# Reordering the last 512 tokens of a Mamba input stage: all convolutions first, two a slot, then the gates

## The chip, the cores and the metric

The kernel runs on one core of a Trainium2 chip. A core has TensorE (PE in the profile; its weight loads are PEld), VectorE (DVE), ScalarE (ACT), GpSimd (POOL), and SyncE (SP), whose queue here issues most of the DMAs. Each engine works through its own instructions in order and waits on semaphores for the others. The metric is the device time of one execution in microseconds; before the change the median of three runs is 3320.36 us (3317.36 to 3326.46).

## The reference, cut to what matters

The whole is one decoder layer over 4 x 1024 tokens of width 512: a Mamba block with an MLP, then a cross attention, then a dense layer with routed low-rank experts. The change lies in the first part of the Mamba block:

```
xz = rmsnorm(x) @ in_proj_w.T
u, z = split(xz, 2)                       # 1024 channels each
u_act = silu(conv4(u) + conv_b)           # causal, 4 taps, per channel
proj = u_act @ x_proj_w.T                 # 32 for dt, 16 for B, 16 for C
dt = softplus(dt_r @ dt_proj_w.T + dt_proj_b)
dA = exp(dt * A);  dBu = dt * B * u_act   # 16 states per channel
h_t = dA_t * h_{t-1} + dBu_t;  y = sum_n h * C + u_act * D
y = y * silu(z);  out = y @ out_proj_w.T
```

softplus(v) is computed as relu(v) + ln(1 + exp(-|v|)), with the rounding error of the sum 1 + e taken back out.

## The kernel before, in words

The 4096 tokens are cut into eight chunks of 512 (`c` = 0 to 7, `NC` = 8), and the 1024 inner channels into eight blocks of 128 (`j` = 0 to 7, `KI` = 8). There are two stages that matter here.

**The input stage** (`mamba_in`, line 357) makes u, z, dt and dt*u for every chunk and puts them into DRAM as `pk`. It is a software pipeline written out by hand in *slots*, one for each (c, j), numbered 8c + j in what follows. A slot has four phases. `slot(c, j)` (line 630) runs what is due in phase 0, issues the 12 matmuls of `conv(j)`, runs phase 1, issues the 12 matmuls of `gate(j)`, and runs phases 2 and 3. `at(d, phase, f)` puts a step d slots later. The distances stand in the table `AP` at the top of the file.

- `conv(j)` (479): matmuls into PSUM `ps_in`; one slot later ScalarE makes the first tap (`conv_start`, `cv`) and VectorE the other three (`conv_taps`, plus three narrow ones from the `halo` in odd chunks); two slots later ScalarE makes tanh (`conv_tanh`, which takes a new tile `u`, eight buffers, each for two blocks) and VectorE `conv_end`; three slots later comes `x_proj`.
- `gate(j)` (534): matmuls, then tanh on ScalarE and a multiply on VectorE one slot later, and a DMA of z.
- After `x_proj` of the eighth block, `project` (549) copies the projection to `pr` and `bc`, and eight `dt(b)` (574) follow at the distances `AP["b"]`: (2,2), (2,2), (3,2), (3,2), (6,2), (6,3), (7,2), (7,3). Each `dt` is one matmul into one of two PSUM buffers `ps_dt`; one slot later ScalarE makes four passes (`dt_exp`, 598: `e` = |v|, `r` = relu, exp into `ps_dt`, and `q` = 1 + exp), then VectorE makes `dt_round` (607), GpSimd `dt_add` (595). After each four of them ScalarE makes the logarithm (`dt_log`, 610), VectorE `dt_sum`, GpSimd `dt_u` (622), which is the last reader of the tile `u`. `q` and `r` have two buffers, each for four blocks.

So the softplus of chunk 6 falls into slots 60 to 69 and that of chunk 7 into slots 68 to 77. After slot 63 no matmul of `conv` or `gate` is left; the slots 64 to 72 are run alone (`while n < 9`), and the remaining five are handed over as a generator, `rest()` (685).

**The scan** (`scan_mlp`, line 695) then goes through 256 steps (chunk, half of the channels, state), four quarters each. GpSimd makes dt*u*B (`times_b`, tile `hs`), ScalarE exp(dt*A) (`exp`, tile `da`), VectorE the scan itself, TensorE the transposes (`ps_h`), and ScalarE, VectorE or GpSimd the sums over states (`acc`, `hc`, `hz`). The first four steps are interleaved with what is left of the input stage: every other quarter draws one slot of `rest()`. From step 40 on, the output projection and the MLP run beside the scan.

**What sets the order.** All instructions of an engine that come from `mamba_in` keep their program order (`InOrder`, line 291), and so do all of `scan_mlp`; the scheduler may interleave these two sequences by its own estimate of times. DMAs of the SP queue are not held in that order. The scan's tiles `pk` and `b` lie in the memory of the weights `wu`, and the three buffers of `hs` in the memory of `wz`, so that GpSimd's first `hs` must wait for the last `gate` matmul. Every instruction goes through the helper at line 311, so the profile names tiles and not lines.

Of the kernel before, what the change touches and what calls it, by code (L numbers as in the profile page):

```python
# [10 lines left out]
F32 = mybir.dt.float32  # L11
F32R = mybir.dt.float32r
I32 = mybir.dt.int32
AF = mybir.ActivationFunctionType
ALU = mybir.AluOpType
# [4 lines left out]
P = 128  # L20
# [3 lines left out]
DI, KI = 1024, 8  # L24
NS = 16
DTR = 32
T = 512
NT = T // P
NC = N // T
# [3 lines left out]
AP = {  # L33
    "cv": (1, 1),
    "cw": (1, 3),
    "ut": (2, 1),
    "uu": (2, 2),
    "up": (3, 0),
    "zt": (1, 1),
    "zz": (1, 3),  # L40
    "th": (1, 0),
# [99 lines left out]
for g, first in enumerate((4, 6)):  # L141
    for n in range(1, 16):
        for t in range(4):
            i = 4 * (n - 1) + t
# [182 lines left out]
class Slots:  # L327
# [5 lines left out]
    def at(self, d, phase, f, *args):  # L333
        self.due.setdefault((self.now + d, phase), []).append(lambda: f(*args))

    def run(self, phase):
        for f in self.due.pop((self.now, phase), ()):
            f()
# [18 lines left out]
def mamba_in(tc, cn, a, dr, sx):  # L357
# [5 lines left out]
    nc = pin  # L363
    ident, pvec = cn["ident"], cn["pvec"]
    slots = Slots()
    at, run = slots.at, slots.run
    with ExitStack() as ctx:
# [4 lines left out]
        tp = ctx.enter_context(open_pool(tc, "a_t", bufs=2))  # L372
# [66 lines left out]
        class Step:  # L439
# [39 lines left out]
            def conv(self, j):  # L479
# [5 lines left out]
                at(*AP["uu"], self.conv_end, j, cv)  # L485
                at(*AP["up"], self.x_proj, j)

            def conv_start(self, j, ps, cv):
                cv.append(tp.tile([P, T], F32, tag="cv", name="cv", bufs=2))
                nc.scalar.activation(  # L490
                    cv[0], ps, AF.Identity, bias=vec(V_CB + j), scale=vec(V_CW + 4 * j + 3)
                )
# [29 lines left out]
            def x_proj(self, j):  # L522
                if j == 0:
                    self.xp = qp.tile([P, T], F32, tag="xp", name="ps_xp")
                nc.tensor.matmul(
                    self.xp, wxp[:, j], self.u[j // 2][:, j % 2], start=j == 0, stop=j == KI - 1
                )
                if j == KI - 1:
                    at(1, 0, self.project)
                    at(1, 0, self.project_rest)  # L530
                    for b in range(KI):
                        at(*AP["b"][b], self.dt, b)

            def gate(self, j):

# [3 lines left out]
                at(*AP["zz"], self.gate_end, j, z, ps)  # L539

            def gate_tanh(self, j, z, ps):
                z.append(tp.tile([P, T], F32, tag="z", name="z", bufs=2))
                nc.scalar.activation(z[0], ps, AF.Tanh, scale=0.5)

            def gate_end(self, j, z, ps):
# [28 lines left out]
            def dt(self, j):  # L574


                g, i = divmod(j, 2 * 2)
                if i == 0:
                    self.qr[g] = [
                        sp.tile([P, 2 * 2, T], F32, tag=t, name=t, bufs=4 // 2) for t in "qr"  # L580
                    ]
                q, r = (t[:, i] for t in self.qr[g])
                ps = pd.tile([P, T], F32, tag="dt", name="ps_dt")
                nc.tensor.matmul(ps, wdt[:, j * P : (j + 1) * P], self.pr, start=True, stop=True)
                e = []
                at(*AP["d1"], self.dt_exp, j, ps, e, q, r)
                at(*AP["d2"], self.dt_round, ps, e, q)
                at(*AP["d3"], self.dt_add, e, r)
                if i == 2 * 2 - 1:
                    at(*AP["d4"], self.dt_log, g)  # L590
                    for jp in range(2):
                        at(*AP["d5"][jp], self.dt_sum, 2 * g + jp)
                        at(*AP["d6"][jp], self.dt_u, 2 * g + jp)
# [4 lines left out]
            def dt_exp(self, j, ps, e, q, r):  # L598

                e.append(sp.tile([P, T], F32, tag="e", name="e", bufs=3))  # L600
                (e,) = e
                nc.scalar.activation(e, ps, AF.Abs, bias=vec(V_DTB + j))
                nc.scalar.activation(r, ps, AF.Relu, bias=vec(V_DTB + j))
                nc.scalar.activation(ps, e, AF.Exp, scale=-1.0)
                nc.scalar.activation(q, ps, AF.Identity, bias=1.0)

            def dt_round(self, ps, e, q):
                nc.vector.scalar_tensor_tensor(e[0], q, -1.0, ps, ALU.add, ALU.subtract)
# [19 lines left out]
                put(nc, dr, self.c, jp, 1, q)  # L628

        def slot(c, j):  # L630
            run(0)
            if c < NC:
                now[0].conv(j)
            run(1)
            if c < NC:
                now[0].gate(j)
            run(2)
            if c < NC:
                if j == 0 and c + 1 < NC:
                    n = now[1] = Step(c + 1)  # L640
                    for t in range(NT):
                        at(*AP["nm"][t], n.moments, t)
                        at(*AP["nx"][t], n.normed, t)
                    for k in range(KD):
                        at(*AP["t"][k], n.turn, k)
                    at(*AP["nr"], n.scale)
                if later and (c, j) >= WS:
                    Weight(*later.pop(0))
                if j == KI - 1:
                    now.pop(0)  # L650
                    now.append(None)
            run(3)
            slots.now += 1
# [23 lines left out]
                    load_in(wz, DI, j // 3, [nc.gpsimd, nc.vector])  # L677
                slot(c, j)
        assert not later
        n = 0  # L680
        while n < 9:
            slot(NC, n)
            n += 1

    def rest():
        n = 9
        while slots.due:
            slot(NC, n)
            n += 1
            yield  # L690
# [1383 lines left out]
```

## Time and profile before

| | |
|---|---|
| median of three runs | 3320.36 us |
| the profiled execution | 3321.16 us, span 3319.4 us, mean granted TensorE clock 0.955 |
| busy over the span | PE 90%, DVE 86%, POOL 74%, ACT 62% |
| last `conv` matmuls / last `gate` matmuls start | 499.81 us / 503.01 us |
| `project` of chunk 7 on ScalarE | 521.88 us |
| GpSimd's first `hs` / VectorE's first scan | 534.33 us / 536.70 us |
| GpSimd's last `q<-r,u` (the last work of the input stage on it) | 593.46 us |

The shares over the span are averages over stages with different limits: the input stage until about 506 us, a handover between the stages until about 597 us, the scan alone until about 760 us, then the scan with the MLP, and last the attention. The change touches only slots 56 to 77, which is 451.7 us to about 596 us, so that stretch has to be read by itself.

### The profile page before, as it was taken

How to read it: one execution, taken by the hardware profiler on the slowest of the kernel's cores; microseconds unless marked ns; L12 is line 12 of the kernel's file. 1: busy time of each engine (PE TensorE's matmuls, PEld its weight loads, DVE VectorE, ACT ScalarE, POOL GpSimd, SP SyncE). 2: the span in 40 equal slices, each digit the busy share in tenths (PEclk: the TensorE clock that was granted, in tenths of full speed). 3: DMA queues.
4: the chain of work that ended last, by engine and by line, in shares of the span. 5: the costliest groups of instructions: out<-in, count | busy, mean ns of one | idle time of the engine just before them, and what ended most of it. 6: DMA issues, size and time to landing. Idle time of an engine off the chain costs nothing.

```text
span 3319.4 us, 47302 instructions
## 1 busy us (share of the span) xinstructions
PE 2993.0 (90%) x15768; PEld 2366.4 (71%) x15768; DVE 2867.0 (86%) x4063; ACT 2043.6 (62%) x4000; POOL 2454.5 (74%) x2153
## 2 busy tenths in 40 slices
PE   7999894677899999999999998999999998999986
PEld 5767672565686786786786786786786887998875
DVE  6888887998999999999999999999983346889887
ACT  3778788775665566665566665566652336666642
POOL 1456547898999999999999999999972215667643
PEclk9999995678999999999999999999999999999998
DMA  4677745334666666666766765765757532112010
GB/s 161 221 260 241 256 175 173 99 111 166 210 207 193 216 203 191 222 203 188 230 196 184 238 190 183 241 191 179 234 171 231 161 108 93 52 39 65 30 39 32
DMA packets 478474, 562.79 MB, mean 170 GB/s; under 512 B 46006, under 2 KB 309814, under 8 KB 477974
## 3 DMA queue, kind: packets, MB, share of 16 engines
q1 hardware_dynamic: 464406, 526.21, 49.6%
q10 hardware_dynamic: 13824, 33.56, 2.9%
q8 instruction: 125, 2.05, 0.2%
q14 instruction: 119, 0.97, 0.1%
HBM read 430.18 MB, written 129.50 MB: 169 GB/s over the span
## 4 chain that ended last, share of the span: by engine, by line
PE 38%; DVE 26%; POOL 10%; issue 6%; ACT 5%; DMA 3%; SPq 0%; ACTq 0%; POOLq 0%; DVEq 0%
DVE hs L311 11%; PE ps_ab L311 10%; PE ps_h L311 5%; PE ps_o L311 5%; POOL hs L311 5%; PE ps_m L311 5%; DVE acc L311 5%; PE ps_s L311 3%; PE ps_b L311 2%; POOL acc L311 2%; DVE g L311 1%; ACT da L311 1%; PE ps_in L311 1%; PE ps_y L311 1%; PE ps_num L311 1%
## 5 line engine op out<-in xcount | busy, mean ns | idle before, releaser
L311 DVE TENSOR_TENSOR_SCAN hs<-da,hs 128x512 f32<-128x512 f32 x1024 | 1225.3, 1217 | 19.8 <-ACT da L311 19.4
L311 POOL TENSOR_TENSOR hs<-pk,b 128x1024 f32<-128x1024 f32 x512 | 1214.1, 2387 | 23.3 <-PE ps_h L311 14.9
L311 ACT ACTIVATE da<-pk,aneg 128x512 f32<-128x512 f32 x1024 | 706.2, 690 | 632.1 <-DVE hs L311 622.0
L311 PE MATMUL ps_ab<-xn,w 128*128 128x512 f32 x3072 | 832.6, 407 | 3.4 <-DVE xs L311 3.4
L311 PE MATMUL ps_h<-ident,hs 128*128 128x128 f32 x4096 | 693.0, 291 | 129.1 <-DVE hs L311 66.1
L311 PEld LDWEIGHTS ps_h<-ident,hs 128*128 128x128 f32 x4096 | 533.4, 148 | 371.0 <-DVE hs L311 112.2
L311 PEld LDWEIGHTS ps_ab<-xn,w 128*128 128x128 f32 x3072 | 547.8, 191 | 98.9 <-DVE xs L311 4.1
L311 DVE SCALAR_TENSOR_TENSOR acc<-ps_h,c,acc 128x512 f32<-128x512 f32 x598 | 439.8, 735 | 26.1 <-PE ps_h L311 20.7
L311 PE MATMUL ps_m<-w,gs 128*128 128x512 f32 x1536 | 418.4, 409 | 6.0 <-POOL gs L311 3.5
L311 POOL TENSOR_TENSOR acc<-acc,hc 128x512 f32<-128x512 f32 x232 | 298.9, 1288 | 68.3 <-ACT hc L311 67.1
L311 PEld LDWEIGHTS ps_m<-w,gs 128*128 128x128 f32 x1536 | 275.6, 192 | 55.4 <-POOL gs L311 5.5
L311 PE MATMUL ps_o<-wo,wy 128*128 128x512 f32 x512 | 247.1, 601 | 10.0 <-DMA wy<-y 8.8
L311 POOL TENSOR_TENSOR gs<-g,gs 128x512 fp32r<-128x512 f32 x128 | 164.9, 1288 | 79.8 <-ACT gs L311 79.5
L311 PE MATMUL ps_in<-xn,wu 128*128 128x512 f32 x768 | 217.5, 433 | 0.3 <-DVE xn L475 0.2
L311 PE MATMUL ps_in<-xn,wz 128*128 128x512 f32 x768 | 193.2, 400 | 8.2 <-DVE cv L311 4.1
L311 ACT ACTIVATE hc<-ps_h,c 128x512 f32<-128x512 f32 x288 | 193.1, 671 | 3.8 <-PE ps_h L311 3.8
L311 PEld LDWEIGHTS ps_in<-xn,wu 128*128 128x128 f32 x768 | 147.4, 193 | 58.8 <-issue 23.8
L311 POOL TENSOR_TENSOR pt<-pw,pt 128x512 fp32r<-128x512 f32 x48 | 67.3, 1402 | 161.8 <-ACT pt L311 133.8
L311 PEld LDWEIGHTS ps_in<-xn,wz 128*128 128x128 f32 x768 | 143.2, 189 | 43.4 <-ACT q L311 4.6
L311 DVE SCALAR_TENSOR_TENSOR g<-g,ps_ab 128x512 f32<-128x512 f32 x128 | 87.4, 683 | 85.3 <-ACT g L311 84.7
L311 DVE SCALAR_TENSOR_TENSOR cv<-ps_in,pvec,cv 128x509 f32<-128x509 f32 (+2 forms) x192 | 143.3, 746 | 4.8
L311 POOL TENSOR_TENSOR q<-qf,q 128x256 fp32r<-128x256 f32 x64 | 47.6, 744 | 127.4 <-ACT q L311 127.3
(251 smaller groups left out, 4982.6 us busy)
## 6 DMA issues: line engine op xcount, KB each, us to landing
w<-w SPq DMA_DIRECT2D x384, 512.0 KB, 5.3
b<-b SPq DMA_DIRECT2D x256, 256.0 KB, 4.3
pk<-pk SPq DMA_DIRECT2D x64, 512.0 KB, 5.8
w<-pt SPq DMA_DIRECT2D x48, 512.0 KB, 3.1
pk<-z SPq DMA_DIRECT2D x64, 256.0 KB, 2.3
pk<-u SPq DMA_DIRECT2D x32, 512.0 KB, 3.7
pk<-r SPq DMA_DIRECT2D x32, 512.0 KB, 4.6
pk<-q SPq DMA_DIRECT2D x32, 512.0 KB, 5.3
```

Source lines behind the costliest of these rows:

```text
L311: ins = f(*args, **kw)
```

## The change

In the last chunk (slots 56 on) the order of `conv` and `gate` changes. Slots 56 to 59 issue two `conv` each, slots 60 to 67 one `gate` each, in the place of one `conv` and one `gate` in each of the slots 56 to 63. Since two convolutions are under way at once, those with odd j take their `cv` tile from the two buffers of `z`, and the odd gates their `z` from those of `cv` (`tile`). The eight `dt` of chunk 6 come two a slot in slots 60 to 63 (they were in 60, 60, 61, 61, 64, 64, 65, 65). `project` of chunk 7 comes in slot 64, two slots after its last `x_proj`, and its `dt` come two a slot in slots 65 to 68 (they were in 68, 68, 69, 69, 72, 72, 73, 73). In chunks 6 and 7, `q` = 1 + e moves from ScalarE (`dt_exp`) to VectorE (`dt_one`). The slots run alone after slot 63 are five (64 to 68) in the place of nine, and the rest is four slots (69 to 72) in the place of five (73 to 77).

```diff
+            def tile(self, tag, other, j):
+                if self.c == NC - 1 and j % 2:
+                    tag = other
+                return tp.tile([P, T], F32, tag=tag, name=tag, bufs=2)
...
-                cv.append(tp.tile([P, T], F32, tag="cv", name="cv", bufs=2))
+                cv.append(self.tile("cv", "z", j))
...
-                    at(1, 0, self.project)
-                    at(1, 0, self.project_rest)
+                    last = self.c - (NC - 2)
+                    at(2 if last == 1 else 1, 0, self.project)
+                    at(2 if last == 1 else 1, 0, self.project_rest)
                     for b in range(KI):
-                        at(*AP["b"][b], self.dt, b)
+                        at(*(AP["b"][b] if last < 0 else (2 + last + b // 2, 2 + b % 2)), self.dt, b)
...
-                z.append(tp.tile([P, T], F32, tag="z", name="z", bufs=2))
+                z.append(self.tile("z", "cv", j))
...
                 at(*AP["d1"], self.dt_exp, j, ps, e, q, r)
+                if self.c >= NC - 2:
+                    at(*AP["d2"], self.dt_one, ps, q)
                 at(*AP["d2"], self.dt_round, ps, e, q)
...
-                nc.scalar.activation(q, ps, AF.Identity, bias=1.0)
+                if self.c < NC - 2:
+                    nc.scalar.activation(q, ps, AF.Identity, bias=1.0)
+            def dt_one(self, ps, q):
+                nc.vector.tensor_scalar(q, ps, 1.0, None, ALU.add)
...
         def slot(c, j):
+            i = KI * (c - (NC - 1)) + j
             run(0)
-            if c < NC:
+            if i < 0:
                 now[0].conv(j)
+            elif i < KI // 2:
+                now[0].conv(2 * i)
             run(1)
-            if c < NC:
+            if i < 0:
                 now[0].gate(j)
+            elif i < KI // 2:
+                now[0].conv(2 * i + 1)
+            elif i < KI // 2 + KI:
+                now[0].gate(i - KI // 2)
...
-                if j == KI - 1:
+                if j == KI - 1 and c + 1 < NC:
                     now.pop(0)
...
-        n = 0
-        while n < 9:
+        for n in range(5):
             slot(NC, n)
-            n += 1
...
-        n = 9
+        n = 5
```

## The prediction

> **What bounds the kernel now.** I read the page's 40 slices first, to find the stage; then the busy time by stage; then the timeline around the end of the slots; last GpSimd's groups in the handover. The slices show the dip that the change is aimed at (the seventh slice, 498 to 581 us):
>
> ```profile
> PE   7999894677899999999999998999999998999986
> DVE  6888887998999999999999999999983346889887
> ACT  3778788775665566665566665566652336666642
> POOL 1456547898999999999999999999972215667643
> PEclk9999995678999999999999999999999999999998
> ```
>
> The stretches 451.7 to 506 (slots 56 to 63), 506 to 534.3 (until GpSimd's first hs), 534.3 to 597 (the first scan steps, mixed with the rest of the input stage), and 597 to 760 (scan alone); columns are busy us per engine, granted clock, DMA share:
>
> ```profile
> 451.70:506.00 54.30, 53.98 (x221) 40.89 (x220) 47.24 (x77) 46.00 (x70) 22.28 (x16) 1.00 0.40 148
> 506.00:534.30 28.30, 9.38 (x18) 3.77 (x17) 13.88 (x18) 22.81 (x36) 16.61 (x9) 0.58 1.01 335
> 534.30:597.00 62.70, 27.28 (x94) 17.98 (x95) 54.12 (x45) 44.77 (x71) 57.71 (x35) 0.50 0.26 89
> 597.00:760.00 163.00, 128.65 (x728) 99.64 (x727) 159.76 (x160) 131.68 (x251) 153.49 (x74) 0.72 0.33 105
> ```
>
> TensorE is the limit to 506 (54.0 of 54.3), ScalarE with its chain of softplus in the second row (22.8 of 28.3), GpSimd in the third (57.7 of 62.7), VectorE in the fourth (159.8 of 163). GpSimd's timeline shows where the scan is held:
>
> ```profile
> 527.55 5.57 POOL L311 TENSOR_TENSOR q<-r,u 128x1024 f32<-128x1024 f32 x2 [3.44 <-DVE r L311]
> 533.09 1.27 POOL L311 TENSOR_TENSOR r<-r,e 128x512 f32<-128x512 f32 x1
> 534.33 13.88 POOL L311 TENSOR_TENSOR hs<-pk,b 128x1024 f32<-128x1024 f32 x6
> 548.17 3.72 POOL L311 TENSOR_TENSOR r<-r,e 128x512 f32<-128x512 f32 x3
> ```
>
> The groups of 534 to 598 (busy us and mean ns, then idle before and its releaser) show what the handover costs GpSimd, and VectorE's sums beside it:
>
> ```profile
> L311 POOL TENSOR_TENSOR hs<-pk,b 128x1024 f32<-128x1024 f32 x15 | 34.8, 2339 | 0.0
> L311 POOL TENSOR_TENSOR q<-r,u 128x1024 f32<-128x1024 f32 x4 | 10.3, 2583 | 5.0 <-DVE r L311 5.0
> L311 POOL TENSOR_TENSOR r<-r,e 128x512 f32<-128x512 f32 x8 | 10.0, 1262 | 0.0
> L311 DVE TENSOR_TENSOR r<-r,q 128x1024 f32<-128x1024 f32 x4 | 15.6, 3926 | 3.0 <-issue 3.0
> ```
>
> The first hs has no wait before it: it stands in GpSimd's queue behind chunk 6's last dt_u and a dt_add, not behind memory (the last gate matmuls were over at 505.97). From there GpSimd hardly rests until 595.89, where its steady row of hs begins. So the change is worth what it does to two things: when the first hs can start, and how much dt_add and dt_u is left for GpSimd after that.
>
> **The conv slots, 56 to 59.** The matmuls are the same 24 a slot, 5.6 us by the chain (two pieces of 2.8), so TensorE gains nothing here. VectorE pays: one conv is 2.31 (three taps) + 0.73 (halo) + 0.69 (conv_end) = 3.7 us, two are 7.5, against 4.4 for a conv and a gate (0.68). Its chain, from the conv_end at 457.82, where slot 57 begins: slot 57, 0.7 + 6.1 (taps and halo of two) + 1.4 (two dt_round of chunk 5) = 8.2; slot 58, 1.4 + 6.1 + 1.4 = 8.9; slot 59, 0.7 (project_rest) + 1.4 + 6.1 = 8.2, to 483. ScalarE has 7.9 in slot 58 and 8.5 in slot 59 beside it, of which 4.5 is the logarithm of chunk 5 with two table loads (500.17 to 504.69 shows one).
>
> **A new wait in slot 60.** `u` has eight buffers. The third tile of chunk 7 is now taken in slot 60, phase 1, by conv_tanh(4), and it needs the buffer whose last reader is chunk 5's dt_u(2), in slot 60, phase 2. Before, it was taken two slots later. dt_u(2) needs dt_sum(2) on VectorE (483 to 484.2), then 2.4 to 3.3 on GpSimd: about 487. Behind the waiting tanh on ScalarE stand the first taps of conv 6 and 7, for which VectorE waits. Then two conv_end, one stretched by GpSimd (2.85 in the timeline at 505.75, against 0.69), 3.5 us, and 6.1 of taps: 497. Without the wait it would be 494.
>
> **The gate slots, 60 to 67, and both softplus.** ScalarE sets the pace. One dt costs it 0.57 + 0.71 + 0.63 = 1.9 from start to start (before: 2.42 with q), one z 0.5, project 1.1, a logarithm 4.5. From 497: slot 61 tanh 0.6, z, two dt, 0.1: 5.0; slot 62, 4.3; slot 63 with a logarithm, 8.8; slot 64 with project, 5.4; slot 65, z and logarithm, 5.0; slot 66, 4.3. Sum 32.8, so the second dt of chunk 7 leaves ScalarE at 529.8. Then 1 + e and dt_round on VectorE (1.35), the dt matmul that waits for this PSUM buffer in TensorE's queue (0.3), and behind it the last gate, 2.8: over at 534.3 at full clock. That releases `wz`, so hs can start. GpSimd has by then chunk 6's dt_u (logarithm over at 524, sums, then 3.3 + 2.4 with one dt_add between) and dt_add of the first two dt.
>
> **The clock.** After the TensorE gap from 509.8 the granted clock was 0.55, and the dt matmul there took 0.80 in the place of 0.40. In slot 63 TensorE has about 3.3 of work in 8.8 us, so one or two gates run at half clock: 5.1 in the place of 2.8 (12 x 0.43). I count 1.7 us for that: first hs at 536. The Trainium skill, "TensorE: Matmul & The Clock Gate", section "What's actually happening", has the clock halved after an idle window of about 3.4 us and given back after as long a busy one; by that rule most gate slots, whose gaps are shorter, stay fast, and the sum would be 534 to 537. It speaks against thinning out the matmuls, as this change does, but not by much.
>
> **1 + e on VectorE.** No row shows this form (PSUM in, SBUF out). TENSOR_SCALAR on 128x512 from SBUF took 0.59 (x<-x,rms_r), a pass with a PSUM input 0.68 (z<-z,ps_in): 16 x 0.59 to 0.68 = 9.4 to 10.9 us onto VectorE, I take 0.6, since there is one input. ScalarE loses 16 x 0.598 = 9.6. Eight of these are in the gate slots, where VectorE has at most 6.4 a slot; of the others four come after 536, 2.4 us, in a stretch where VectorE was busy 54.1 of 62.7 and 11 of its 15.6 us of r<-r,q were stretching (1.2 alone, up to 7.45 beside GpSimd). If GpSimd stopped being the limit there, 2.4 us would be the price. The skill's "SBUF — State Buffer", "Who interferes with whom", says that only a VectorE instruction with two SBUF inputs, or in a two-port mode, is locked out by GpSimd; 1 + e has one input, in PSUM, so by it 0.6 holds. By the stretched row it could be several us.
>
> **DMAs.** The counts are the same: eight z, four u, eight r and eight q puts for the two chunks. The z puts come later, the pk and b loads can come earlier, since `wu` is free after slot 59. The stretch 506 to 534.3 had the DMA engines full (1.01), so that is spread out, for nothing gained: hs did not wait for it. One edge is sharper: chunk 6's second q buffer is put at about 535, a put lands in 5.3 us, and dt_one(4) of chunk 7 writes that buffer at about 537. If it waits, VectorE's queue stands for up to 4 us, with scans behind it. I put nothing, GpSimd being the limit.
>
> **Sum.** First hs at 536 against 534.33: +1.7. Behind it GpSimd has the same 14 hs, the same four dt_u (10.3) and six dt_add in the place of seven: -1.25. ScalarE's rest falls from 19.8 (five dt, two logarithms, part of a dt) to about 14.5, off the path. That is +0.4 on the profiled 3321.16, so 3321.6; the median lies 0.8 below that execution: 3321. Bounds of the first hs: if ScalarE never waited from 457.15 on (26.5 + 32.8, then 4.5), 521, 13 us earlier; if all gates ran at half clock (five slots without a logarithm 1.3 to 2.4 longer, some 10) and the q wait came too (4), 550.
>
> **Rivals.** *Faster:* no wait for `u` (the scheduler may put dt_sum before the taps) and no drop of the clock, the gate slots following the matmuls as closely as ScalarE allows: first hs 521 to 526, -8 to -13, 3309. For it: in 451.7 to 597 no engine is over 80% busy on the whole, so there is slack to take. Against: VectorE's 7.5 a conv pair. *Slower:* TensorE stays at half clock through the gates. A gate of 5.1 and two dt of 0.8 are 6.7 a slot, more than ScalarE's 4.3 to 5.4; it decides when more than three gates are slow, and gives +10 to +14, 3333. For it: 600 to 650 shows a clock of 0.5 to 0.67 with TensorE busy 70 to 83%, so it need not recover. Against: 660 to 690 shows 1.00 at 78 to 83%. *No effect of moving 1 + e:* ScalarE's 9.6 us are given to waits; this ends where the forecast does.
>
> **How the numbers follow.** Forecast (3321, its own range 3312 to 3329) 0.44; faster 0.28; slower 0.28. A difference under 0.3%, 10 us, is about what a measurement of this kernel can't tell from no change; the forecast's range lies inside it and the rivals mostly outside. The range reaches a little past the rivals' values: 3304 to 3338.
>
> **What would show it.** Right: VectorE without gaps until about 483; ScalarE waiting for GpSimd before a tanh near 485; the last taps over near 497; first hs 533 to 539; hs in steady rows from 594 to 599. Wrong: the first hs before 528, or gates of over 4 us in most slots, or r<-r,q stretched in slots 64 to 67, or a scheduler that puts the scan's work in front of the softplus.

## The result, and the profile after

The changed kernel takes 3339.24 us (median of five runs, 3337.55 to 3339.48), the kernel before 3320.36 beside it: 18.9 us more, a ratio of 1.0055 (95% interval 1.0043 to 1.0066). The forecast was 3321 with a range to 3338. The profiled execution after has a span of 3337.1 us, against 3319.4.

Three rows of the 40 slices of the page after (busy tenths of TensorE and GpSimd, granted clock):

```profile
PE   6999894687899899999999999999999998999986
POOL 1465536997999999999999999999972215667643
PEclk9999996578899999999999999999999999999998
```

TensorE's dip is still there. A slice is 83 us long, so these rows can't show more; from the middle on they are those of before. The stretches of the kernel after by engine (busy us with counts for PE, PEld, DVE, ACT and POOL, then granted clock, DMA share, GB/s); the first is that of before, the second ends with the first hs:

```profile
451.70:506.00 54.30, 42.10 (x150) 28.50 (x148) 47.13 (x77) 34.88 (x55) 16.67 (x13) 0.91 0.35 130
506.00:562.20 56.20, 29.86 (x93) 20.00 (x93) 33.18 (x40) 43.06 (x61) 30.22 (x19) 0.77 0.55 192
562.20:611.00 48.80, 23.94 (x87) 16.12 (x88) 40.70 (x38) 26.91 (x44) 48.80 (x27) 0.50 0.35 126
```

Before, TensorE was busy 54.0 of the first 54.3 us; now 42.1, and ScalarE has fallen too (46.0 to 34.9). GpSimd is saturated in the third row, as predicted, but that row begins 28 us later than before. GpSimd's timeline after shows the handover (start, duration, instruction, idle time before it and what ended that):

```profile
544.60 2.53 POOL L311 TENSOR_TENSOR r<-r,e 128x512 f32<-128x512 f32 x2
549.97 1.26 POOL L311 TENSOR_TENSOR r<-r,e 128x512 f32<-128x512 f32 x1 [2.83 <-DVE e L311]
555.98 1.28 POOL L311 TENSOR_TENSOR r<-r,e 128x512 f32<-128x512 f32 x1 [4.75 <-DMA c<-c]
558.88 3.26 POOL L311 TENSOR_TENSOR q<-r,u 128x1024 f32<-128x1024 f32 x1 [1.62 <-DMA pk<-pk]
...
562.24 14.86 POOL L311 TENSOR_TENSOR hs<-pk,b 128x1024 f32<-128x1024 f32 x6
```

The first hs starts at 562.24, against 534.33 before. Ahead of it stand a sum and a product of chunk 7's softplus, and two waits that the profile puts down to DMAs. The first was not a wait for the DMA named. The sum reads `e`, which VectorE finished 0.14 us before the sum began, and ScalarE had made the exponential for it behind its own wait for a load of `pk`:

```profile
552.50 1.30 ACT L311 ACTIVATE da<-pk,aneg 128x512 f32<-128x512 f32 x2 [3.29 <-DMA pk<-pk]
553.75 0.58 ACT L311 ACTIVATE ps_dt<-e 128x512 f32<-128x512 f32 x1
```

So the scan's first step held up the softplus (ScalarE's `da` ahead of the exponential of chunk 7's sixth dt), and this softplus then held up the first hs. The product at 558.88 likewise began 0.07 us after VectorE's sum for it had ended.

**GpSimd's work and idle time.** Up to the start of the twentieth hs all of the input stage's work on GpSimd is done, in the kernel before as in the one after, so this point closes the same list of GpSimd's work. Here is the stretch from 451.7 to it, of the kernel before:

```profile
451.70:607.50 155.80, 98.06 (x365) 67.89 (x364) 125.73 (x149) 122.41 (x193) 107.11 (x63) 0.70 0.46 158
```

and of the kernel after:

```profile
451.70:622.80 171.10, 105.71 (x367) 71.36 (x365) 132.78 (x166) 114.98 (x177) 107.49 (x64) 0.72 0.41 145
```

GpSimd's work is the same, 107.1 and 107.5 us. Its idle time is not: 155.8 - 107.1 = 48.7 before, 171.1 - 107.5 = 63.6 after. The twentieth hs comes 15.3 us later, and 14.9 of that is idle time of GpSimd. From there on both kernels run alike: the 64th scan is 15.0 us later (660.4 against 645.4), the 1024th and last scan 16.4, the span 17.7 us longer. What is settled by the twentieth hs is most of the difference.

By stretches, before against after: up to 506 us 54.3 - 22.28 = 32.0 against 54.3 - 16.67 = 37.6; from there to the first hs 28.3 - 16.61 = 11.7 against 56.2 - 30.22 = 26.0; behind the first hs 5.0 against none. That is +5.6, +14.3 and -5.0. The experiments had to show what makes these.

### The profile page after: what moved, and what is told of

It reads as the page before. It is cut to its first block, busy times and chain, and to the rows that moved or that the text cites. A ratio compares the mean times of both kernels' runs of the same rounds, so it can differ in the third digit from the quotient of the medians.

```text
span 3337.1 us, 47331 instructions
## 1 busy us (share of the span) xinstructions
PE 3010.5 (90%) x15768; PEld 2378.2 (71%) x15768; DVE 2872.0 (86%) x4079; ACT 2037.9 (61%) x3984; POOL 2457.1 (74%) x2153
## 4 chain that ended last, share of the span: by engine, by line
PE 43%; DVE 29%; POOL 9%; ACT 7%; issue 7%; DMA 4%; SPq 1%; ACTq 0%; DVEq 0%; POOLq 0%
DVE hs L311 11%; PE ps_ab L311 10%; PE ps_o L311 6%; PE ps_h L311 6%; PE ps_m L311 5%; DVE acc L311 5%; PE ps_in L311 5%; POOL hs L311 4%; PE ps_s L311 3%; PE ps_b L311 2%; DVE g L311 2%; DVE cv L311 1%; ACT da L311 1%; PE ps_y L311 1%; POOL acc L311 1%
## 5 line engine op out<-in xcount | busy, mean ns | idle before, releaser
L311 DVE SCALAR_TENSOR_TENSOR cv<-ps_in,pvec,cv 128x509 f32<-128x509 f32 x180 | 134.4, 746 | 4.5
```

The lines of the kernel that those rows point to most:

```text
L311: ins = f(*args, **kw)
```

## The experiments

Three theories stood at the start. A: waits and the order of the queues make the last gate late, and with it the loads and the first hs. B: 1 + e makes VectorE the limit. C: GpSimd's chain of sums and products sets the end, whatever the first hs does.

The profiled executions do not reach the changed part at the same time, although they run the same instructions up to it. ScalarE's first tap of the last block of chunk 6 (slot 56) stands ahead of everything that is changed. Here it is in the kernel before, and in the changed kernel with `r - e` on VectorE, the run in which it is earliest:

```profile
453.95 0.76 ACT L311 ACTIVATE cv<-ps_in,pvec 128x512 f32<-128x512 f32 x1
...
449.69 0.76 ACT L311 ACTIVATE cv<-ps_in,pvec 128x512 f32<-128x512 f32 x1
```

The difference of this tap to 453.95 is called the shift of a run; it lies between -4.3 and 1.7 us, as much as many of the effects. It has to be taken off: less the shift, the last tanh of the convolutions ends at 500.0 to 500.1 us in all nine changed kernels with eight `u`, and at 497.6 in all four with ten. In the table the dates and the lag of scan 32 (604.2 us in the kernel before) are less the shift. Idle is GpSimd's idle time from this tap to the twentieth hs (from the tap on and not from 451.7, so 46.5 and 61.5 in the place of 48.7 and 63.6). The ratio is to the kernel before, beside which each ran. Dates and idle times are of one execution for each kernel; the medians are of 4 to 10 (five for the changed kernel).

| kernel | shift | last gate over | first hs | scan 32 lag | GpSimd idle | median, us | ratio (95%) |
|---|---|---|---|---|---|---|---|
| before | 0 | 506.0 | 534.3 | 0 | 46.5 | 3320.36 | 1 |
| after | 0.4 | 545.2 | 561.9 | 14.6 | 61.5 | 3339.24 | 1.0055 (1.0043, 1.0066) |
| before, 1 + e on VectorE | 1.2 | 506.0 | 532.7 | 2.2 | 46.7 | 3321.53 | 1.0001 (0.9992, 1.0010) |
| after, 1 + e on ScalarE | 0.3 | 548.2 | 561.0 | 17.3 | 64.0 | 3340.50 | 1.0060 (1.0045, 1.0075) |
| ten `u` | 1.7 | 544.4 | 559.2 | 11.9 | 58.4 | 3333.28 | 1.0037 (1.0022, 1.0051) |
| loads by ScalarE's queue | -0.8 | 545.9 | 555.8 | 14.2 | 60.2 | 3335.58 | 1.0044 (1.0029, 1.0059) |
| `q` elsewhere | -0.2 | 543.6 | 558.6 | 14.1 | 60.3 | 3338.35 | 1.0047 (1.0032, 1.0062) |
| ten `u`, `q` elsewhere | 1.2 | 540.6 | 556.7 | 12.2 | 58.0 | 3334.75 | 1.0033 (1.0021, 1.0046) |
| gates two a slot | 0.4 | 521.7 | 535.6 | 4.2 | 53.1 | 3328.62 | 1.0021 (1.0011, 1.0030) |
| the same, ten `u`, `q` elsewhere | -1.3 | 519.2 | 533.2 | 8.3 | 53.2 | 3331.35 | 1.0029 (1.0017, 1.0041) |
| short gates | -3.0 | 542.0 | 553.9 | 12.3 | 58.5 | 3334.71 | 1.0040 (1.0025, 1.0055) |
| gates two a slot, ten `u` | 1.1 | 519.3 | 533.2 | 11.4 | 55.9 | 3333.34 | 1.0031 (1.0019, 1.0044) |
| before, dt of chunk 6 two a slot | -0.2 | 506.4 | 539.9 | 3.0 | 48.5 | 3323.49 | 1.0005 (0.9995, 1.0014) |
| the same, 1 + e on VectorE | -2.5 | 506.5 | 539.8 | 1.7 | 48.4 | 3321.07 | 0.9999 (0.9990, 1.0009) |
| gates two a slot, late dt of chunk 7 | -2.2 | 521.7 | 534.3 | 8.5 | 53.4 | 3331.88 | 1.0034 (1.0022, 1.0046) |
| gates two a slot, nine slots alone | -1.2 | 521.7 | 535.6 | 4.2 | 53.1 | 3328.22 | 1.0027 (1.0016, 1.0038) |
| after, `r - e` of chunk 7 on VectorE | -4.3 | 546.3 | 560.0 | 11.7 | 66.8 | 3335.03 | 1.0049 (1.0031, 1.0067) |
| before, `r - e` of chunk 7 on VectorE | -0.5 | 506.0 | 533.1 | -5.1 | 49.1 | 3317.22 | 0.9988 (0.9979, 0.9998) |

GpSimd's busy time in this stretch lies between 106.9 and 109.7 us in the first sixteen rows, so what a row loses, it loses in the idle column but for 2.7 us at most. A lag of 2 to 3 us at scan 32 with a median equal to that of before (1 + e on VectorE, dt of chunk 6) shows how little such a lag can prove.

### 1 + e alone, and without it

In the kernel before, this alone (the guard and `dt_one` of the change):

```diff
+                if self.c < NC - 2:
                     nc.scalar.activation(q, ps, AF.Identity, bias=1.0)
+            def dt_one(self, ps, q):
+                nc.vector.tensor_scalar(q, ps, 1.0, None, ALU.add)
...
+                if self.c >= NC - 2:
+                    at(*AP["d2"], self.dt_one, ps, q)
                 at(*AP["d2"], self.dt_round, ps, e, q)
```

> The kernel before with one part of the change alone: in chunks 6 and 7, 1 + e is made by VectorE (dt_one) and no longer by ScalarE. Theory A (the loss comes from waits that the new order makes: the wait for a u buffer 8.45 us, the waits for the put of q 2.87 and 1.46 us, and the late loads of pk, 16.6 us between the last gate and the first hs): this part alone costs nothing, 3312 to 3322 us, since ScalarE has 2.42 us for one dt and VectorE is idle half of 506 to 534. Rival B (VectorE carries too much, two conv a slot and the 16 passes of 0.69 us): slower by the passes that fall into the scan's first steps, 5 x 0.69 = 3.5 us and more, 3324 to 3332.

And the changed kernel with `q` = 1 + e back in `dt_exp`:

```diff
-                if self.c < NC - 2:
-                    nc.scalar.activation(q, ps, AF.Identity, bias=1.0)
+                nc.scalar.activation(q, ps, AF.Identity, bias=1.0)
...
-                if self.c >= NC - 2:
-                    at(*AP["d2"], self.dt_one, ps, q)
```

> The changed kernel with 1 + e back on ScalarE in all chunks; the new order stays. Theory A: the waits stay and ScalarE gets 16 x 0.6 = 9.6 us more in the gate slots, where it is near the limit: 3339 to 3349. Rival B: VectorE is relieved of 11 us: 3328 to 3334.

Alone it does nothing (1.0001, interval to 1.0010), and without it the change costs what it costs with it (1.0060 against 1.0055, the intervals overlap). The instruction itself, in the group of VectorE from 451 to 606 us of the first of the two (busy, mean ns, idle before):

```profile
L311 DVE TENSOR_SCALAR q<-ps_dt 128x512 f32<-128x512 f32 x16 | 11.0, 689 | 9.7 <-ACT ps_dt L311 9.7
```

Theory B falls.

### The wait for `u`

```diff
-open_pool(tc, "a_u", bufs=8, side="right")
+open_pool(tc, "a_u", bufs=10, side="right")
```

> The changed kernel with ten buffers for u in the place of eight, so that conv_tanh(4) of chunk 7 has no need to wait for chunk 5's dt_u. Theory A: the 8.45 us wait on ScalarE goes, the taps of conv 6 and 7 start some 5 us earlier, and 3 to 7 us of it reach the end: 3332 to 3336. Rival B: VectorE was idle for only 2.93 us there, and that is then lost to the next wait: 3337 to 3340.

The wait was there, as predicted. ScalarE's timeline after:

```profile
490.13 0.63 ACT L311 ACTIVATE u<-cv 128x512 f32<-128x512 f32 x1 [8.45 <-POOL q L311]
...
496.85 0.63 ACT L311 ACTIVATE u<-cv 128x512 f32<-128x512 f32 x1 [4.23 <-DVE cv L311]
499.82 0.63 ACT L311 ACTIVATE u<-z 128x512 f32<-128x512 f32 x1 [2.34 <-DVE z L311]
```

and with ten buffers:

```profile
485.30 0.63 ACT L311 ACTIVATE u<-cv 128x512 f32<-128x512 f32 x1
...
495.67 0.63 ACT L311 ACTIVATE u<-cv 128x512 f32<-128x512 f32 x1 [6.29 <-DVE cv L311]
498.67 0.63 ACT L311 ACTIVATE u<-z 128x512 f32<-128x512 f32 x1 [2.36 <-DVE z L311]
```

8.45 us of wait are gone, and the last tanh of the convolutions comes 1.15 us earlier, 2.5 less the shifts: VectorE's taps were late next, and ScalarE's wait for them grew from 4.23 to 6.29. Less the shifts, the last gate is 0.8 us earlier, the first hs and scan 32 are 2.7 us earlier. The median is 6 us lower, but the two intervals overlap. So this wait explains some 3 of the 14.6 us at scan 32.

### The loads behind the queue

SyncE's queue after (start, time to issue, line, transfer):

```profile
544.68 0.52 SPq L354 DMA_DIRECT2D pk<-q  x1
545.29 2.18 SPq L751 DMA_DIRECT2D pk<-pk  x3
...
551.05 1.98 SPq L760 DMA_DIRECT2D b<-b  x3
```

The first four `pk` loads stand behind a put of `q` that needs GpSimd's product. Their memory, that of `wu`, was free with the last conv matmul at 487.3. Moving these four to ScalarE's queue:

```diff
-            def load(self, jp, q):
+            def load(self, jp, q, eng=nc.sync):
...
-                nc.sync.dma_start(pk, dr["pk"][self.c][2 * self.half + jp][:, :, q])
+                eng.dma_start(pk, dr["pk"][self.c][2 * self.half + jp][:, :, q])
...
-                step(0).load(jp, i)
+                step(0).load(jp, i, nc.scalar)
```

> The changed kernel with the scan's first four loads of pk issued from ScalarE's queue in the place of SyncE's, where they stood behind puts of q and z until 545.29 us. Theory A: the loads are there before the last gate is over (545.6), ScalarE's first da does not wait (3.29 us), the first hs comes 4 to 12 us earlier than 562.2, and the time is 3328 to 3335. Rival B: the first hs stands behind dt_u in GpSimd's queue anyway: 3337 to 3340.

GpSimd's timeline of this run:

```profile
549.50 1.26 POOL L311 TENSOR_TENSOR r<-r,e 128x512 f32<-128x512 f32 x1 [3.10 <-DVE e L311]
555.08 2.35 POOL L311 TENSOR_TENSOR hs<-pk,b 128x1024 f32<-128x1024 f32 x1 [4.32 <-DMA pk<-pk]
...
559.59 3.32 POOL L311 TENSOR_TENSOR q<-r,u 128x1024 f32<-128x1024 f32 x1
...
563.00 4.66 POOL L311 TENSOR_TENSOR hs<-pk,b 128x1024 f32<-128x1024 f32 x2
```

Less the shifts the first hs comes 6.0 us earlier, and only that one: the second starts at 563.0, behind a product of chunk 7, and scan 32 gains 0.4 us. The loads were issued at 545.1 again, since on ScalarE they stand behind the last gate's tanh; so what an earlier issue would give was not tried. The run shows that the date of the first hs by itself is not what counts.

### The wait for `q`

The first `q` of chunk 7 in the memory of the token tile `x`, which the input stage no longer needs by then:

```diff
+xp.tile([P, 2 * 2, T], F32, tag="x", name="q")
+if t == "q" and self.c == NC - 1 and g == 0
+else sp.tile([P, 2 * 2, T], F32, tag=t, name=t, bufs=4 // 2)
```

> The changed kernel; the first q tile of chunk 7 lies in the memory of the token tile x, which is free by then, so that dt_one(0) of chunk 7 need not wait for the put of chunk 6's q (2.87 us at 538.1). Theory A (waits in the queues add up): the last gate comes 3 to 4 us earlier (542 in the place of 545.6), and the time is 3334 to 3337. Rival C (the path is ScalarE's and GpSimd's chain of the softplus, the last gate does not matter): within 1 us of the change, 3338 to 3340.

And together with the ten `u`:

> The changed kernel with both: ten u buffers and the q tile in the memory of x. Theory A: the gains of the two add up, 6 and 3 us: 3328 to 3332. Rival C: as with ten u buffers alone, 3332 to 3335.

The wait is VectorE's, in the timeline after:

```profile
538.14 0.69 DVE L311 TENSOR_SCALAR q<-ps_dt 128x512 f32<-128x512 f32 x1 [2.87 <-DMA pk<-q]
```

Less the shifts, the last gate is 1.7 us earlier without it, scan 32 0.5. Both together gain 4.6 at the last gate and 2.4 at scan 32. But these two runs do not price the wait. With `q` in that memory, ScalarE's second `acc` of the scan waits for the put of `q`:

```profile
583.91 0.69 ACT L311 ACTIVATE acc<-ps_h,c 128x512 f32<-128x512 f32 x1 [12.08 <-DMA pk<-q]
```

In the run with both edits it waits 12.12 us; in the changed kernel the same instruction starts at 575.48 without a wait. The edit removed a wait of 2.87 us and brought one of 12. So theory A in this form is shown too small for `u` alone (2.7 of 14.6 us); for `q` it stays open.

### Gates two a slot

The gates as dense as the convolutions, in slots 60 to 63 (`dt` and the rest as changed):

```diff
             elif i < KI // 2:
                 now[0].conv(2 * i)
+            elif i < KI:
+                now[0].gate(2 * i - KI)
...
-            elif i < KI // 2 + KI:
-                now[0].gate(i - KI // 2)
+            elif i < KI:
+                now[0].gate(2 * i - KI + 1)
```

> The changed kernel with the eight gates issued two a slot in slots 60 to 63 and none after; all else as changed. Theory A (the last gate, which stands in TensorE's queue behind the dt matmuls and frees the memory for the scan, is too late): the last gate is over at 522 to 530 in the place of 545.6, the first hs comes at 540 to 550, and the time is 3322 to 3332. Rival C: the last gate comes as early, but GpSimd's dt_add and dt_u still stand before the first hs: 3335 to 3340.

This is the one edit that undoes more than half: 10.6 us in the median, the last gate 23.5 us earlier, scan 32 10.3. Its stretches:

```profile
451.70:506.00 54.30, 47.26 (x175) 33.13 (x173) 47.18 (x77) 34.84 (x55) 16.62 (x13) 0.94 0.36 135
506.00:536.00 30.00, 18.43 (x63) 12.74 (x63) 18.78 (x23) 22.31 (x31) 13.61 (x10) 0.80 0.60 198
536.00:611.00 75.00, 36.33 (x125) 23.71 (x126) 70.15 (x66) 56.26 (x89) 73.84 (x41) 0.50 0.46 151
```

GpSimd's idle time from 451.7 on is 37.7 up to 506 us, 16.4 to the first hs and 1.2 behind it, 55.2 in all; against the kernel before +5.7, +4.7 and -3.8. So the part up to 506 us is untouched by the gates. It is the same as after, and is looked at below.

With the ten `u` and the other `q` added:

> The same with ten u buffers and the q tile in the memory of x. Theory A: 5 to 9 us less than with two gates a slot alone, 3314 to 3324. Rival C: at most 3 us less than it.

Less the shift the first hs is 1.1 us earlier than in the kernel before, and scan 32 is 8.3 us later. GpSimd's timeline shows where:

```profile
542.00 9.26 POOL L311 TENSOR_TENSOR hs<-pk,b 128x1024 f32<-128x1024 f32 x4
551.23 1.25 POOL L311 TENSOR_TENSOR r<-r,e 128x512 f32<-128x512 f32 x1
...
578.29 4.68 POOL L311 TENSOR_TENSOR hs<-pk,b 128x1024 f32<-128x1024 f32 x2
```

Between 551 and 578 there is no hs at all: the softplus's list has got in one piece ahead of the scan's. This, too, comes with the moved `q`: ScalarE's second `acc` waits for its put until 577.04 here, 4.93 us, and VectorE's next scan for ScalarE until 578.34. So this run can't show what an early first hs is worth. Others can: with the loads by ScalarE's queue it was 6.0 us earlier, and scan 32 only 0.4; with the dt of chunk 6 two a slot (below) it is 5.5 us later, and the time is that of before. The date of the first hs by itself does not count. Theory C is right on that.

### TensorE's clock

The eight gates of chunk 7 with 4 matmuls in the place of 12:

```diff
+        if short:
+            nc.tensor.matmul(ps, w[0][:, k, s], xn[0][k], start=k == 0, stop=k == KD - 1)
+            continue
         mm3(
...
-                ps = in_proj(nc, pp, wz, j * P, self.xn)
+                ps = in_proj(nc, pp, wz, j * P, self.xn, self.c == NC - 1)
```

> The changed kernel, with the gates of chunk 7 made by 4 matmuls in the place of 12 (only the first of the three products; the multiplier z of the last chunk is less exact by this). Eight gates of 3 to 4 us lose 2 to 2.7 us of TensorE each, and the tanh that waited 4.1 us for one of them has nothing to wait for. Theory 'TensorE at half clock makes the last gate late': the last gate is over at 533 to 537 in the place of 545.6, the first hs comes at 548 to 553, time 3328 to 3332. Theory 'the lists and waits of the other engines make it late, TensorE only follows': only the last gate's own 2.7 us are saved, over at 541 to 544, first hs 558 to 561, time 3335 to 3339.

TensorE's timeline after shows what there was to gain:

```profile
493.19 1.98 PE L311 MATMUL ps_xp<-u,wxp 128*128 128x512 f32 x4 [0.91 <-DVE u L311]
...
504.23 0.80 PE L311 MATMUL ps_dt<-pr,wdt 96*128 96x512 f32 x1 [5.80 <-DVE e L311]
...
506.63 3.48 PE L311 MATMUL ps_xp<-u,wxp 128*128 128x512 f32 x4
509.26 3.64 PE L311 MATMUL ps_in<-xn,wz 128*128 128x512 f32 x12
...
513.19 2.96 PE L311 MATMUL ps_in<-xn,wz 128*128 128x512 f32 x12
...
519.05 7.32 PE L311 MATMUL ps_in<-xn,wz 128*128 128x512 f32 x24
...
539.61 0.79 PE L311 MATMUL ps_dt<-pr,wdt 96*128 96x512 f32 x1 [7.15 <-DVE e L311]
...
541.53 4.08 PE L311 MATMUL ps_in<-xn,wz 128*128 128x512 f32 x12
```

Behind a gap of 5.8 and of 7.2 us a dt matmul takes 0.8, and the next gate 3.6 and 4.1; four matmuls of `x_proj` behind the first gap take 3.48 in the place of 1.98. A gate at full clock takes 2.96 to 3.36. The Trainium skill, "TensorE: Matmul & The Clock Gate", section "What's actually happening", has the clock halved after an idle window of some 3.4 us and given back after a busy one; the two long gaps agree with it.

The two gates from 519.05 on, which take 7.32 together, are another case. Here the granted clock fell to 0.50 for 3.4 us although no gap ahead of it was over 1.1 us. The first row is the stretch before the drop, the second the drop (busy us as above, granted clock, DMA share, GB/s):

```profile
516.67:520.08 3.41, 1.86 (x7) 1.33 (x8) 1.89 (x3) 3.38 (x3) 2.54 (x2) 1.00 0.01 2
520.08:523.50 3.42, 3.42 (x10) 2.65 (x9) 3.03 (x3) 3.39 (x6) 1.77 (x2) 0.50 0.19 70
```

TensorE was not idle in the first row, but busy 1.86 of 3.41 us. An idle window, as the page has it, does not cover this drop: in this trace matmuls thinned out to about half were enough.

With the short gates the last one is over 3.3 us earlier less the shifts, of which 2.2 are its own (4.08 to 1.91); the first hs is 7.9 earlier, scan 32 gains 2.2, the median 4.5 with overlapping intervals. The last gate, at 542.0, is where the second theory had it; the first hs and the time lie between the two. TensorE's time, slow or not, is a part of the late gate, not the main one.

### What is left with gates two a slot

The ten `u` again, without the other `q`:

> The changed kernel with the gates two a slot in slots 60 to 63 and ten buffers of u (without q in the memory of x). If the two savings that were measured alone add up (10.6 and 6 us), 3322 to 3324, with the first hs at 528 to 532 and scan 32 by 605. If what follows the first hs sets the end (GpSimd's list of sums and products of chunk 7 between the scan's first steps), scan 32 stays at 608 to 611 and the time at 3327 to 3331, wherever the first hs is.

3333.34, and 1.0031, above both ranges: the savings do not add up, and less the shifts scan 32 is 7.2 us later than with the gates two a slot alone. The trace shows why. GpSimd's order is the same in both runs until its last product of the softplus, and this run is ahead by 1.8 us (583.07 against 584.87 for the same `da` on ScalarE). Then one instruction of ScalarE differs. With gates two a slot:

```profile
595.87 0.67 ACT L311 ACTIVATE hz<-ps_h,c 128x512 f32<-128x512 f32 x1
```

and with the ten `u`:

```profile
606.28 0.69 ACT L311 ACTIVATE hz<-ps_h,c 128x512 f32<-128x512 f32 x1 [12.14 <-POOL q L311]
```

`hz` waits 12.14 us for GpSimd's last product, and VectorE's scan stands 9.55 us behind it. That two more buffers of `u` put `hz` into memory which this product still reads fits the wait, but is not shown. As with `q`, an edit that takes a wait away has brought another one.

The dt of chunk 6 two a slot, alone in the kernel before:

```diff
-                        at(*AP["b"][b], self.dt, b)
+                        at(*((2 + b // 2, 2 + b % 2) if self.c == NC - 2 else AP["b"][b]), self.dt, b)
```

> The kernel before, with one part of the change alone: the eight dt of chunk 6 two a slot in slots 60 to 63. ScalarE gets 14 us more (four dt of 2.4 and a logarithm of 4.5) ahead of the last gate, where it was busy 46.0 of 54.3: the last gate some 6 us later, 512. Behind it 14 of ScalarE's 22.8 us are gone. If the first hs sets the time: it comes at 522 to 527, time 3310 to 3315. If GpSimd's list from the first hs to the last q<-r,u sets it, which this makes shorter by no more than GpSimd's idle time of 506 to 534 (11.7 us): 3313 to 3320. If the softplus only pushes the convs and gates back as it does in the changed kernel: last gate 516 or later, first hs 534 or later, time 3320 to 3328.

and with 1 + e on VectorE besides:

> As the run before, and 1 + e of chunks 6 and 7 on VectorE. ScalarE has 4.8 us less ahead of the last gate. If ScalarE sets the last gate there: last gate 2 to 5 us earlier than in that run, and the time 2 to 5 us shorter. If VectorE (47.2 of 54.3 busy, and 5.3 more by this) or TensorE sets it: no difference, within 2 us.

Both equal the kernel before (1.0005 and 0.9999), with a first hs that is 5.5 us later. The last gate stays at 506.4 and 506.5 us, against an expected 512: with its convs and gates in the old order TensorE isn't held up by the softplus. So two of the parts of the change cost nothing that can be measured in the old order, even together.

Then, on the gates two a slot, chunk 7's softplus back in its old slots:

```diff
-                    at(2 if last == 1 else 1, 0, self.project)
+                    at(5 if last == 1 else 1, 0, self.project)
...
-                        at(*(AP["b"][b] if last < 0 else (2 + last + b // 2, 2 + b % 2)), self.dt, b)
+                        d, p = AP["b"][b]
+                        at(*((d + 4, p) if last == 1 else (d, p) if last < 0 else (2 + b // 2, 2 + b % 2)), self.dt, b)
...
-        for n in range(5):
+        for n in range(9):
...
-        n = 5
+        n = 9
```

> The changed kernel with the gates two a slot in slots 60 to 63, project and the eight dt of chunk 7 in the slots that they had before (67, and 68 to 73) and nine slots alone. The conv order, the dt of chunk 6 and 1 + e stay as changed. If chunk 7's early softplus is what costs the last 7 to 10 us of the run with two gates a slot: scan 32 at 602 to 606, time 3317 to 3324. If the conv order itself costs them (a last gate at 518 to 522 in the place of 506): first hs 534 to 540, scan 32 at 607 to 611, time 3326 to 3331.

and the cut of the handover alone (the last two edits of that diff, on the gates two a slot):

> The changed kernel with the gates two a slot in slots 60 to 63, and nine slots run alone in the place of five, so that nothing of the input stage is handed to the scan's steps. If the cut sets the order in which chunk 7's softplus and the first scan steps are taken: the first hs behind most of that softplus, 545 or later, the last q<-r,u before 585, and a time off by more than 4 us from the run with five alone. If the scheduler merges the two sequences by its own estimate wherever the cut is: the same as with five alone, 3326 to 3331, first hs 532 to 540.

Neither gives back what is left (1.0034 and 1.0027, against 1.0021 with overlapping intervals): not the date of chunk 7's softplus, and not the cut. What all runs with the convolutions first have in common is GpSimd's idle time early on. From the tap that marks the shift to 52.05 us behind it (506.0 in the kernel before) it is 35.6 to 35.9 us with eight `u` and 33.9 to 34.1 with ten, against 29.7 to 30.4 in the five with the old order. The kernel before and the one after differ there in when ScalarE reaches the first dt of chunk 6. Before:

```profile
486.55 0.69 ACT L311 ACTIVATE e<-ps_dt,pvec 128x512 f32<-128x512 f32 x1
```

After:

```profile
500.83 0.68 ACT L311 ACTIVATE e<-ps_dt,pvec 128x512 f32<-128x512 f32 x1
```

It is 14.3 us later (13.9 less the shift), behind the taps and tanh of the last two convolutions. GpSimd gets its first sum of chunk 6 at 504.31 in the place of 490.56.

### Is it GpSimd's list?

If GpSimd's list sets the stretch, work taken off it must shorten both kernels. The eight `r - e` of chunk 7 on VectorE:

```diff
-                nc.gpsimd.tensor_tensor(r, r, e[0], ALU.subtract)
+                eng = nc.vector if self.c == NC - 1 else nc.gpsimd
+                eng.tensor_tensor(r, r, e[0], ALU.subtract)
```

In the changed kernel:

> The changed kernel with the eight r - e of chunk 7 (128x512, 1.26 us each on GpSimd) on VectorE. Two of the eight stand behind the first hs, some four between 538 and 560. Theory 'GpSimd's list sets the stretch up to the scan's steady row': its work up to the twentieth hs falls from 107.5 by some 10 us; those that lay in idle time give nothing, so scan 32 and the end come 3 to 8 us earlier, 3331 to 3336. Theory 'the softplus chain sets it (ScalarE and the sums), GpSimd follows': its idle time grows by what is taken away, scan 32 stays at 617 to 621, time 3336 to 3342.

In the kernel before:

> The kernel before with the eight r - e of chunk 7 on VectorE: there seven of them stand behind the first hs, in a stretch in which GpSimd rests 5.0 of 62.7 us. Theory 'GpSimd's list sets the stretch': the last q<-r,u and the steady row come 5 to 8 us earlier, scan 32 at 596 to 600, time 3312 to 3316. Theory 'the softplus chain sets it': scan 32 at 603 to 606, time 3319 to 3323. If VectorE's sums, stretched beside GpSimd (r<-r,q 3.9 us in the mean there), become the limit: later than before, scan 32 at 606 to 612, time 3322 to 3328.

In the changed kernel the median is 3335.03 (1.0049, 1.0031 to 1.0067), and this interval overlaps that of the kernel without the edit. Scan 32 comes 7.5 us earlier (611.6), but 4.6 of that are the shifts; 2.9 remain, at the edge between the theories. GpSimd has 8.3 us less work and 5.3 us more idle time. The two of the eight sums that stood behind the first hs are 2.5 us, about what arrives; the others left idle time behind.

In the kernel before, where seven of them stand behind the first hs, scan 32 comes 5.1 us earlier less the shift, and the median is 3317.22 against 3319.77: a ratio of 0.9988 (0.9979 to 0.9998), a little above the time that was expected of it. The seven are 8.8 us, of which 5.1 arrive. Part of the rest went into GpSimd's own hs, which took 2.54 us in the mean in the place of 2.34, while VectorE's `r<-r,e` took 2.08. The groups of that run from 534 to 598 us, GpSimd's first:

```profile
L311 POOL TENSOR_TENSOR hs<-pk,b 128x1024 f32<-128x1024 f32 x17 | 42.7, 2535 | 0.0
...
L311 DVE TENSOR_TENSOR r<-r,e 128x512 f32<-128x512 f32 x7 | 14.4, 2081 | 0.0
...
L311 DVE TENSOR_TENSOR r<-r,q 128x1024 f32<-128x1024 f32 x4 | 4.7, 1203 | 0.0
```

So work taken off GpSimd's list made scan 32 earlier where it stood behind the first hs, and turned into idle time where it stood ahead of it. That the list sets the stretch behind the first hs fits both runs, and GpSimd's 48.80 busy of 48.80 us there. It is not proved: the edit also takes GpSimd out of the softplus chain between VectorE's rounding and its sum, and a shorter chain would act in the same direction. The second kernel is the only one that beats the kernel before, and by little.

## Why the prediction was wrong

**Conv slots.** Right: TensorE's matmuls gained nothing, and VectorE's chain set the slots.

**The wait in slot 60.** Right as to place, engine and end (tanh at 490.1, forecast 487; last tanh at 499.8, taps forecast 497). Its cost was forecast at 3 us; taking it away made the last tanh 2.5 us earlier (less the shifts) and scan 32 2.7, so the size was right too.

**The gate slots and the last gate.** Forecast: second dt of chunk 7 off ScalarE at 529.8, last gate over at 534.3. Measured: 536.1 and 545.6. The 11.3 us are 6.3 up to ScalarE's dt (2.7 from the taps, the rest with a wait of 4.1 for a gate in ScalarE's list, 512.93 in its timeline), then 3.7 until the gate starts (VectorE stood 2.87 for the put of `q`, and a second dt matmul stands ahead of the gate), then 1.3 of a slow gate. The clock, for which 1.7 was set, has some 3.5 of this by an estimate from the rows above: 1.3 here, and 1.5 + 0.7 in the wait of 4.1, since the `x_proj` matmuls (3.48 against 1.98) and the gate (3.64 against 2.96) ahead of that tanh ran in part at half clock. It was mis-sized by half, but the waits are the larger part.

**The `q` wait.** Forecast at `dt_one(4)` and set at nothing, "GpSimd being the limit". It came at the first dt of chunk 7 with 2.87 us, where the last gate's dt matmul hung on it, and once more with 1.46 at 548.42. Taking it away gave 1.7 us at the gate less the shifts; what it costs at the end is open, since that edit brought a wait of its own.

**The step that failed: "First hs at 536 against 534.33: +1.7".** It was 562.24, +27.9: 11.3 from the late gate, and 16.6 us between the last gate and hs, where the sum had nothing. There the loads of `pk` and `b`, written down as "can come earlier", were issued at 545 to 553, behind a put in SyncE's queue. ScalarE's first `da` waited for one of them until 552.50, and chunk 7's softplus behind it, so that GpSimd's next sum started at 555.98 and its product held GpSimd until 562.14. "For nothing gained: hs did not wait for it" was read from before and carried over to a kernel where it no longer held: with the loads by ScalarE's queue the first hs waits for `pk` itself (4.32 us).

**The work behind it: "-1.25".** Also far off, the other way: the twentieth hs was only 15.3 us later, so 12.6 of the 27.9 were given back. With the first hs late, most of chunk 7's sums were already done. The two errors belong together. The prediction split GpSimd's work at the first hs and summed the two sides, but the first hs is only one item in a list of some 107 us. The sum that holds is that list plus GpSimd's idle time, and there the change adds 14.9 us of the latter. The prediction never counted GpSimd's idle time ahead of the first hs, although the rows it showed had 32.0 and 11.7 us of it.

**1 + e.** Right: no effect either way; the upper price of 0.68 holds, not 0.6 (0.689 measured, of 16). The Trainium skill's "SBUF — State Buffer", "Who interferes with whom", says that a VectorE instruction with at most one SBUF input, outside the two-port modes, does not contend with GpSimd; 1 + e has its input in PSUM, and its 0.66 to 0.69 us in all runs agree.

**The rivals.** "TensorE stays at half clock, 3333" came nearest in time, but not by its mechanism: it counted 5.1 us for a slow gate and decides when more than three are slow. By TensorE's timeline the eight gates took 27.5 us together, the slowest 4.08, and eight at 2.96 would be 23.7. Of the 3.8 us between, 3.2 belong to the four that ran in part at half clock. "Faster" fails by the last gate.

**What is shown, what is open.** Shown: spreading the gates over eight slots costs about 10 of the 19 us (gates two a slot). The moved dt of chunk 6 and 1 + e cost nothing that can be measured in the old order of conv and gate; putting chunk 7's dt back gained nothing on top of the dense gates. What remains, 7 to 10 us, is then put down to the order of conv and gate itself, by elimination; no run changed that order alone, and what the parts cost only together is not excluded. That it works through the late first dt of chunk 6 (13.9 us) fits GpSimd's idle time early on, 5.7 to 6.0 us more than before in every run with this order and eight `u`, but no run moved that dt alone.

## What to carry to other kernels

When an engine is saturated from some point on, cost a reordering by that engine's whole list plus its idle time before this point, stretch by stretch, and not by the date at which its first late-stage instruction starts. A wait that is removed is worth what the next late engine leaves of it: here 2.5 of 8.45 us. A tile that is given other memory to remove a wait can bring a wait to that memory's next user: here 12 us on ScalarE for a put, in the place of 2.87 on VectorE. And before the late dates of two executions are compared, compare where they stood ahead of the first changed instruction: here they differed by up to 6 us there, and gains of 5.6 and 7.5 us at scan 32 (short gates, `r - e` on VectorE) came down to 2.2 and 2.9.

## What the runs showed of the hardware

- Sums of two SBUF operands on VectorE stretch beside GpSimd, but it is not always the same ones: with `r - e` on VectorE these took 2.08 us in the mean, and `r<-r,q` fell to 1.20 from the 3.93 that it took in the kernel before. GpSimd pays too: its hs took 2.54 us in the mean beside them, 2.34 before. An operation from PSUM (1 + e) stayed at 0.66 to 0.69 in all runs, beside GpSimd or not.
- The granted clock fell to 0.50 for 3.4 us after a stretch of 3.41 us in which TensorE was busy 1.86 us, without a gap over 1.1 us.
